# Layer 1's normalised patches two rows at a time in two buffers, filters and gated products alternating, transposes an iteration ahead of the projections; layer 2's corner weights in a PSUM bank

## The chip, the cores and the metric

One core of a Trainium2 chip runs the whole program, in float32. The metric is the device time of one execution in microseconds, as the median of several. Beside the timed runs there is one profiled execution, whose span and trace are read below. The engines are TensorE (PE, with its weight loads as PEld), VectorE (DVE), ScalarE (ACT), GpSimd (POOL) and SyncE (SP). SP, ACT and POOL issue DMAs.

## What is computed

Four images of 48 channels and 256 x 256 pixels go through four layers. Each layer adds to its input a function of the group-normalised input:

```python
x = x + L0(gn(x))   # 1x1 and 3x3 convolutions, product of 8x8 FFT patches, layer norm, gate, 1x1
x = x + L1(gn(x))
x = x + L2(gn(x))
x = x + L3(gn(x))   # 1x1, 3x3, gelu gate, 1x1, a filter on 8x8 FFT patches
```

The two layers that the change touches, cut to what matters:

```python
def L1(x):
    y = einsum('oc,bchw->bohw', w_in, x)              # 48 -> 288 channels
    f = rfft2(patches(y, 8)) * fft_mask               # a filter per channel on 8x8 patches
    y = unpatch(irfft2(f))
    y = depthwise_conv3x3(y, w_dw)
    x1, x2 = split(y, 2)
    return einsum('oc,bchw->bohw', w_out, gelu(x1) * x2)   # 144 -> 48

def L2(x):
    integ = cumsum(cumsum(x, -1), -2)                 # the table
    off   = conv1x1(gelu(conv3x3(x, w1_off)), w2_off)  # 4 offsets per pixel: a box
    scale = conv1x1(gelu(conv3x3(x, w1_mod)), w2_mod)  # 48 scales per pixel
    A, B, C, D = [bilinear(integ, corner) for corner in box(off)]
    return (A + D - B - C) / (area(off) * scale)
```

## The kernel before

**Two streams.** The program is written as two lists of work. Stream a does layers 0 and 1 of each image in turn, and then layer 3 of all images. Stream b does the first statistics, layer 1's weights in patch form (`patch_weights`), and then layer 2 of all images. Each layer is a Python generator, and `yield n` says that some n units of time have been written down; `run` always continues the stream whose sum of units is lower, so that both lists are mixed into one program. A layer waits until what it needs is written. So layer 2 of an image begins when its layer 1 has ended, and stands beside layer 0 and layer 1 of the next image; layer 2 of the last image stands beside layer 3. In the last loop of an image's layer 1, stream b has nothing to do. A scheduler at build time may then move instructions of one engine past one another, except those marked `pinned`. On the chip every engine takes its instructions in the fixed order that comes out.

Stream a issues its DMAs on SP (helper `dma`, L227), stream b on POOL; the column loads A and B of the convolutions go through SP or ACT. PSUM has eight banks of 128 x 512: stream a has a ring of five, stream b a ring of two and one bank of its own, `p2`.

**Layer 1** has three loops for each image.

1. *Patches times input weights* (L671 to L699), 16 strips of 8 rows in each half of the image. Two DMAs load the strip's rows into `xn`, one for each half of the image. One VectorE `tensor_scalar` (L679) normalises it and puts its pixels in patch order into `xp`. Then 32 matmuls (L688) with `win` follow, and 32 copies into `hs`, one half by VectorE (L693), the other by ScalarE (L695). One DMA stores `hs` (4608 KB) to `hD`. `xn` and `xp` have one buffer each, `hs` has two.
2. *Filter, 3x3 and gate* (L701 to L770), 72 groups of 4 channels. `fetch` loads `hg` (1024 KB) from `hD`, the filters `ct` and the 3x3 weights `tt` and `ht`, a group ahead. Four matmuls filter the group (L736), and their results are copied to `yt` by VectorE (L741) and ScalarE (L743). Six small transfers (`AROUND`) make `yh` from it, the rows that neighbouring patches need. For the group before, four matmuls multiply its patches (L758) and four its neighbours' rows (L759, accumulating); ScalarE's gelu (L762) and VectorE's product (L763) give `gt`, stored to `gD` every second group.
3. *Projection* (L772 to L808), 16 strips of four iterations. An iteration turns three blocks by four transposes each (L795), copies each block with ScalarE (L797) and multiplies it by the output weights (L798) right after its copy; VectorE adds the input `xt` (L800).

**Layer 2** first makes its table of sums. Then it goes through 32 pieces of eight rows for each image. `convolve` (L908) is the 3x3 convolution of a quarter piece, with ScalarE's gelu; `project` (L928) the 1x1 ones. Two quarters share the bank `p2`, and one VectorE addition (L935, 128 x 416) takes both out into `sc`. `boxes` (L946 to L993) makes of it, on VectorE, the corners, the gather's indices `idx`, the 16 weights for each pixel `w4` (L985) and the divisor. `gather` (L1000) issues from POOL 16 indirect DMAs for each tile `V` (three buffers), four to each of the four pixels a partition. `add` multiplies V by its weights in place (L1011, 128 x 3072, VectorE), adds the 16 corners in four halvings (L1013) and divides (L1014). `finish` turns the result on TensorE (L1025) and adds it to the image (L1032).

Of the kernel before, what the change touches and what calls it, by code (L numbers as in the profile page):

```python
# [11 lines left out]
ALU = mybir.AluOpType  # L12
# [176 lines left out]
class Net:  # L189
# [131 lines left out]
    def normalised_weights(self, wb, n, mr, pool):  # L321


        nc = self.nc
        t = self.column_scales(mr, pool)
        W = pool.tile([112, 4, n], F32, name=self.nm("W"), tag="W")
        md = pool.tile([112, 4], F32, name=self.nm("md"), tag="md")
        nc.vector.scalar_tensor_tensor(md[:], t[:, :, 0], -1.0, t[:, :, 1], ALU.mult, ALU.mult)
        mt = pool.tile([112, 4, 106], F32, name=self.nm("mt"), tag="mt")
        ps = self.bank()  # L330
        for g in range(4):
            k = 112 if g < 3 else 96
            nc.vector.tensor_scalar(W[:k, g, :], wb[:k, g, :], t[:k, g, 1:2], None, ALU.mult)
            nc.vector.tensor_scalar(mt[:k, g, :], self.tapsel[:k, g, :], md[:k, g : g + 1], None, ALU.mult)
        for g in range(4):
            k = 112 if g < 3 else 96
            nc.tensor.matmul(ps[:106, :n], mt[:k, g, :], wb[:k, g, :], start=g == 0, stop=g == 3)
        nc.vector.tensor_copy(W[96:106, 3, :], ps[96:106, :n])
        return W
# [318 lines left out]
    def layer1(self, x, mr, y):  # L658
# [4 lines left out]
        with ExitStack() as ctx:  # L663
            w = ctx.enter_context(self.pool("wa", 1))
            sb = ctx.enter_context(self.pool("ba", 2))

            win = w.tile([112, 288], F32, name="win")
            mh = w.tile([112, 2], F32, name="mh")
            xn = w.tile([112, 8, PW], F32, name="xn")
            xp = w.tile([112, 16, 128], F32, name="xp")  # L670
            nc.vector.memset(xn[32:64], 0.0)  # L671
            nc.vector.memset(mh[32:64], 0.0)
            for h in range(2):
                self.dma(win[64 * h : 64 * h + 48], a["L1_w_in"])
                self.dma(mh[64 * h : 64 * h + 48], mr[48 * h : 48 * h + 48])
            for s in range(NS):
                self.load_rows(xn, x, 8 * s, 8, 64)

                nc.vector.tensor_scalar(  # L679
                    xp[:].rearrange("p b (r c) -> p r b c", c=16),  # L680
                    xn[:, :, 1:257].rearrange("p r (b c) -> p r b c", c=16),
                    mh[:, 0:1], mh[:, 1:2], ALU.subtract, ALU.mult,
                )
                hs = sb.tile([128, 4 * NG, 2, 16], F32, name="hs", tag="hs")
                for b in range(16):
                    for h in range(2):
                        ps = self.bank()
                        nc.tensor.matmul(  # L688
                            ps[:, :288], xp[64 * h : 64 * h + 48, b, :], win[64 * h : 64 * h + 48],
                            start=True, stop=True,  # L690
                        )
                        if h:
                            nc.vector.tensor_copy(hs[:, :, h, b], ps[:, :288])  # L693
                        else:
                            nc.scalar.copy(hs[:, :, h, b], ps[:, :288])  # L695
                    if b == 7:
                        yield 13
                self.dma(hD[:, :, s, :], hs[:].rearrange("p (g c) h b -> p g (c h b)", c=4))
                yield 13  # L699
        with ExitStack() as ctx:  # L700
# [12 lines left out]
            todo, gt = None, None  # L713

# [13 lines left out]
            for g in range(NG + 1):  # L728
                if g < NG:
# [4 lines left out]
                    for c in range(4):  # L734
                        ps = self.bank()
                        nc.tensor.matmul(  # L736
                            ps[:].rearrange("p (s n) -> p s n", n=32), ct[:, c, :], hg[:, :, c, :],
                            start=True, stop=True,
                        )
                        if c % 2:  # L740
                            nc.vector.tensor_copy(pick(yt, 128, c), order(ps[:]))  # L741
                        else:
                            nc.scalar.copy(pick(yt, 128, c), order(ps[:]))  # L743
# [6 lines left out]
                if todo is not None:  # L750
                    go, yo, yho, to, ho = todo
                    if go % 2 == 0:
                        gt = sb.tile([128, NS, 4, 32], F32, name="gt", tag="gt")
                    for c in range(2):
                        both = []
                        for q in (c, c + 2):
                            ps = self.bank()
                            nc.tensor.matmul(order(ps[:]), to[:, q, :], pick(yo, 128, q), start=True, stop=False)  # L758
                            nc.tensor.matmul(order(ps[:]), ho[:, q, :], pick(yho, NZ, q), start=False, stop=True)  # L759
                            both.append(ps)  # L760
                        gl = sb.tile([128, 512], F32, name="gl", tag="gl")
                        nc.scalar.activation(gl[:], both[0][:], AF.Gelu)  # L762
                        nc.vector.tensor_mul(  # L763
                            gt[:, :, 2 * (go % 2) + c, :], gl[:].rearrange("p (s n) -> p s n", n=32),
                            both[1][:].rearrange("p (s n) -> p s n", n=32),
                        )
                    if go % 2:
                        self.dma(gD[:, :, go // 2, :], gt[:].rearrange("p s c n -> p s (c n)"))
# [3 lines left out]
        with ExitStack() as ctx:  # L772
# [5 lines left out]
            for h in range(2):  # L778
                self.dma(pr[:, h, 48 * h : 48 * h + 48], a["L1_w_out"][0:96, :])
                self.dma(pr[h:96:2, 2, 48 * h : 48 * h + 48], a["L1_w_out"][96:144, :])  # L780
            for s in range(NS):
                xt = sb.tile([CP, 8, PW], F32, name="xt", tag="xt")
                self.load_rows(xt, x, 8 * s, 8)
                gs = sb.tile([128, 144, 2, 16], F32, name="gs", tag="gs")
                self.dma(gs[:].rearrange("p c h b -> p (c h b)"), gD[:, s].rearrange("p g n -> p (g n)"))
                for j in range(4):
                    pp = self.bank()
                    for q in range(3):
                        pt = self.bank()
                        for b in range(4):  # L790
                            if q < 2:
                                of = gs[:, 0:96, q, 4 * j + b]
                            else:
                                of = gs[:, 96:144, :, 4 * j + b].rearrange("p c h -> p (c h)")
                            nc.tensor.transpose(pt[:96, 128 * b : 128 * b + 128], of, self.ident[:])  # L795
                        gc = sb.tile([96, 512], F32, name="gc", tag=f"gc{q}")
                        nc.scalar.copy(gc[:], pt[:96, :])  # L797
                        nc.tensor.matmul(pp[:CP, :], pr[:, q, :], gc[:], start=q == 0, stop=q == 2)  # L798
                    v = xt[:, :, 1 + 64 * j : 65 + 64 * j].rearrange("p r (b c) -> p b r c", b=4)
                    nc.vector.tensor_add(v, pp[:CP, :].rearrange("p (b r c) -> p b r c", b=4, r=8), v)  # L800
                    if j == 1:
                        yield 10
                for r in range(8):
                    nc.vector.bn_stats(st[:, 8 * s + r, :], xt[:, r, 1:257])
                self.store_rows(y, xt, 8 * s, 8)
                yield 10
# [67 lines left out]
    def layer2(self, x, mr, y, table):  # L874
# [3 lines left out]
        with ExitStack() as ctx:  # L878
# [15 lines left out]
            centre = self.load("c_centre", [128, 2, 512], w)  # L894
            kk = [112, 112, 112, 106]
# [26 lines left out]
            def project(t, j):  # L922

                if j % 2 == 0:
                    t.p2 = self.banks[self.stream].tile([128, 512], F32, name=self.nm("ps"), tag="p2", bufs=1)
                for b in range(4):
                    n = 52 * (4 * (j % 2) + b)
                    m = nc.tensor.matmul(  # L928
                        t.p2[:, n : n + 52], t.hm[j][:, 128 * b : 128 * b + 128], w2[:], start=True, stop=True
# [3 lines left out]
                if j % 2:  # L933
                    h = j // 2
                    self.pinned(nc.vector.tensor_add(  # L935
                        t.sc[:, 8 * h : 8 * h + 8, :], t.p2[:, 0:416].rearrange("p (k e) -> p k e", e=52),
                        b2[:].unsqueeze(1).to_broadcast([128, 8, 52]),
                    ))

            def boxes(t):  # L940
# [40 lines left out]
                w4 = sb.tile([128, 16, 4, 2, 2], F32, name="w4", tag="w4")  # L981
# [353 lines left out]
```

## Time and profile before

| what | value |
|---|---|
| median of 3 runs | 21125.43 us (21119.59 to 21126.28) |
| profiled execution | 21086.85 us |
| its span in the trace | 21084.9 us |
| layer 1 of image 0: loops 1, 2, 3 | 1971-2290, 2301-3185, 3203-3540 us |
| layer 1 of image 1: loops 1, 2, 3 | 5766-6245, 6262-7416, 7435-7775 us |
| layer 1 of image 2: loops 1, 2, 3 | 10015-10500, 10515-11686, 11704-12043 us |
| layer 1 of image 3: loops 1, 2, 3 | 14282-14770, 14781-15959, 15978-16317 us |
| layer 3 of three images beside layer 2 of the last | about 16430-20034 us |
| DMA | 3440 MB, mean 163 GB/s |

How to read it: layer 1 takes about 1.6 ms of an image without layer 2 beside it (image 0), and 2.0 ms with it. The times are those of one execution, from the span's start. A group's line gives the line number, the engine, the operation, the tile written and the tiles read, the shapes and the count; then busy us and the mean ns of one; then the idle time just before its instructions and what ended it. In a line of waits stand us in total, times, and the longest. In the timeline stand start and duration in us. "PEclk" or the granted clock is the share of TensorE's full clock that it was given. DMA share is the mean busy share of the 16 DMA engines.

### The profile page before, as it was taken

What the parts mean: (1) busy time and instruction counts of PE and PEld (TensorE: products, weight loads), DVE (VectorE), ACT (ScalarE), POOL (GpSimd) and SP (SyncE); (2) the same over time, 40 slices, a digit from 0 to 9 for tenths busy, and PEclk for the clock granted to TensorE, in tenths of its full rate; (3) what the DMA queues carried; (4) which work ended last, traced back from release to release, by engine and by line L of the source; (5) the groups of instructions that cost most, each with busy time, mean ns of one, the idle gap of its engine ahead of it and who ended that gap; (6) DMA issues with size and microseconds to landing.
All of it is one profiled execution on the core that took longest, in us unless ns stands there. A gap on an engine that the chain in (4) does not pass through costs nothing.

```text
span 21084.9 us, 230708 instructions
## 1 busy us (share of the span) xinstructions
PE 18992.2 (90%) x79032; PEld 12013.7 (57%) x79032; DVE 10675.3 (51%) x21479; ACT 5921.8 (28%) x12275; POOL 9864.3 (47%) x8887
## 2 busy tenths in 40 slices
PE   7998898999888879998888799997887899999999
PEld 4565434666443346665433466654334787878888
DVE  4544322476665534766655347667453245555521
ACT  2334212343331123433311234333112211111111
POOL 1000000277775602787755117777552067777700
PEclk9898899999868999999689999996889999999999
DMA  4624885555499955554989655549896566766633
GB/s 115 136 52 102 240 217 166 136 127 132 120 269 231 248 169 137 129 127 119 267 226 240 187 132 126 130 120 252 231 235 195 143 146 153 158 154 157 151 77 74
DMA packets 2420311, 3440.17 MB, mean 163 GB/s; under 512 B 573959, under 2 KB 1990895, under 8 KB 2302460
## 3 DMA queue, kind: packets, MB, share of 16 engines
q1 hardware_dynamic: 1883640, 2084.48, 38.2%
q0 software_dynamic: 452560, 1110.45, 21.4%
q10 hardware_dynamic: 82944, 230.48, 4.5%
q8 instruction: 635, 10.40, 0.2%
q14 instruction: 532, 4.35, 0.1%
HBM read 2486.99 MB, written 802.77 MB: 156 GB/s over the span
## 4 chain that ended last, share of the span: by engine, by line
PE 64%; DMA 12%; POOL 10%; DVE 5%; issue 5%; ACT 2%; SPq 1%; ACTq 0%; DVEq 0%; POOLq 0%
PE ps L426 20%; POOL V L1000 10%; PE ps L908 6%; PE ps L736 5%; PE ps L434 4%; PE ps L798 4%; PE ps L759 3%; DMA ct<-cD 3%; PE ps L758 3%; PE ps L1151 2%; PE ps L688 2%; DMA yh<-ys 2%; PE ps L847 2%; DMA A<-x 1%; ACT gc L797 1%
## 5 line engine op out<-in xcount | busy, mean ns | idle before, releaser
L1000 POOL DMA_INDIRECT V<-t,idx x8192 | 9453.9, 1154 | 3754.0 <-issue 2390.7
L426 PE MATMUL ps<-W,A 128*128 128x288 f32 (+1 forms) x24576 | 5574.7, 376 | 125.5 <-ACT o L531 45.6
L426 PEld LDWEIGHTS ps<-W,A 128*128 128x128 f32 x24576 | 4296.6, 192 | 1275.8 <-issue 517.7
L227 POOL DMA_DIRECT2D X<-x x192 | 145.1, 760 | 4408.7 <-DMA x<-xt 3129.8
L1013 DVE TENSOR_TENSOR V<-V 128x1536 f32<-128x1536 f32 (+3 forms) x2048 | 1841.2, 899 | 20.9
L1011 DVE TENSOR_TENSOR V<-V,w 128x3072 f32<-128x3072 f32 x512 | 1716.5, 3353 | 233.4 <-DMA V<-t,idx 213.0
L736 PE MATMUL ps<-hg,ct 128*128 128x512 f32 x2304 | 1255.2, 695 | 392.0 <-DMA ct<-cD 267.2
L908 PE MATMUL ps<-A,W 112*96 112x512 f32 x3072 | 1543.1, 641 | 13.9 <-DVE xt L1032 13.9
L507 ACT COPY qkv<-ps 128x288 f32<-128x288 f32 x2048 | 769.1, 401 | 2673.0 <-PE ps L426 1262.1
L759 PE MATMUL ps<-yh,ht 65*128 65x512 f32 x2304 | 1191.6, 663 | 207.8 <-DMA yh<-ys 190.8
L688 PE MATMUL ps<-win,xp 48*128 48x288 f32 x4096 | 1022.7, 578 | 336.5 <-DVE xp L679 168.1
L434 PE MATMUL ps<-W,B 58*128 58x288 f32 (+1 forms) x8192 | 1281.4, 392 | 29.7 <-DVE t L518 12.3
L530 DVE BATCH_NORM_STATS2 bs<-ps 128x6 f32<-128x96 f32 x2048 | 394.8, 251 | 1721.2 <-PE ps L528 1721.0
L1131 DVE TENSOR_TENSOR gp<-gl,ps 128x192 f32<-128x192 f32 x1024 | 353.5, 351 | 1672.7 <-ACT gl L1130 1671.9
L763 DVE TENSOR_TENSOR gt<-gl,ps 128x512 f32<-128x512 f32 x576 | 395.4, 687 | 1546.6 <-PE ps L759 1546.5
L736 PEld LDWEIGHTS ps<-hg,ct 128*128 128x128 f32 x2304 | 500.9, 225 | 1085.3 <-issue 1008.9
L758 PE MATMUL ps<-ys,tt 128*128 128x512 f32 x2304 | 1075.9, 608 | 9.1 <-ACT ys L743 9.1
L1130 ACT ACTIVATE gl<-ps 128x192 f32<-128x192 f32 x1024 | 333.5, 331 | 2539.1 <-PE ps L426 2220.0
L434 PEld LDWEIGHTS ps<-W,B 58*128 58x128 f32 x8192 | 765.9, 187 | 465.7 <-issue 355.5
L688 PEld LDWEIGHTS ps<-win,xp 48*128 48x128 f32 x4096 | 631.3, 253 | 694.1 <-ACT hs L695 211.8
L798 PE MATMUL ps<-gc,pr 96*96 96x512 f32 x1536 | 791.7, 625 | 210.4 <-ACT gc L797 195.8
L759 PEld LDWEIGHTS ps<-yh,ht 65*128 65x128 f32 x2304 | 459.0, 203 | 875.8 <-issue 770.1
(186 smaller groups left out, 24304.9 us busy)
## 6 DMA issues: line engine op xcount, KB each, us to landing
hD<-hs SPq DMA_DIRECT2D x64, 4608.0 KB
hg<-hD SPq DMA_DIRECT2D x288, 1024.0 KB
gD<-gt SPq DMA_DIRECT2D x144, 1024.0 KB
gs<-gD SPq DMA_DIRECT2D x64, 2304.0 KB
V<-t,idx POOLq DMA_INDIRECT x8192
A<-x SPq DMA_DIRECT2D x512, 193.5 KB
xt<-x SPq DMA_DIRECT2D x256, 387.0 KB
A<-x ACTq DMA_DIRECT2D x512, 193.5 KB
```

What stands on the lines that cost most here:

```text
L426: nc.tensor.matmul(to(q, b), A[:, r + q, 128 * b + g : 128 * b + g + 128], W[:, g, :], start=b == 0 and g == 0, stop=b == 1 and g == 2,)
L434: nc.tensor.matmul(to(q, b), B[p, r // 2, 128 * b : 128 * b + 128], W[p, 3, :], start=b == 1, stop=b == 0)
L507: nc.scalar.copy(t.qkv[:, 2 * q + b, :], banks[2 * b + q][:, 0:288])
L688: nc.tensor.matmul(ps[:, :288], xp[64 * h : 64 * h + 48, b, :], win[64 * h : 64 * h + 48], start=True, stop=True,)
L736: nc.tensor.matmul(ps[:].rearrange("p (s n) -> p s n", n=32), ct[:, c, :], hg[:, :, c, :], start=True, stop=True,)
L758: nc.tensor.matmul(order(ps[:]), to[:, q, :], pick(yo, 128, q), start=True, stop=False)
L759: nc.tensor.matmul(order(ps[:]), ho[:, q, :], pick(yho, NZ, q), start=False, stop=True)
L798: nc.tensor.matmul(pp[:CP, :], pr[:, q, :], gc[:], start=q == 0, stop=q == 2)
L908: m = nc.tensor.matmul(ps[:96, :].rearrange("p (r c) -> p r c", c=256), W[: kk[g], g, :], of[: kk[g]], start=g == 0, stop=g == 3,)
L1000: nc.gpsimd.indirect_dma_start(out=V[:, k, 4 * cr : 4 * cr + 4, :].rearrange("p e c -> p (e c)"), out_offset=None, in_=table, in_offset=ba ...
L1011: self.pinned(nc.vector.tensor_mul(Vm, Vm, wm.unsqueeze(2).to_broadcast([128, 64, 48])))
L1013: nc.vector.tensor_add(V[:, :, 0:n, :], V[:, :, 0:n, :], V[:, :, n : 2 * n, :])
```

## The change

In layer 1's first loop `xn` becomes two buffers of two rows, `xp` two buffers of a whole strip. A strip's rows are loaded and normalised in four steps of two rows (eight DMAs and four `tensor_scalar` where there were two and one), and the next strip's are written down in the middle of a strip. In the second loop, two filters, two gated products, two filters and two gated products of the group before take turns, and the `yh` transfers come after both. In the third loop the transposes of an iteration are written ahead of the projection of the iteration before. In layer 2 every quarter's projection has a bank of the ring and its own addition (128 x 208), and the bank that was `p2` holds two sets of the weights `w4`. `normalised_weights` takes `mt` from a pool that it gives back. The pieces' operations are otherwise as they were.

```diff
-            xn = w.tile([112, 8, PW], F32, name="xn")
-            xp = w.tile([112, 16, 128], F32, name="xp")
+            xns = [w.tile([112, 2, PW], F32, name=self.nm("xn")) for _ in range(2)]
+            xps = [w.tile([112, 16, 128], F32, name=self.nm("xp")) for _ in range(2)]
...
+            def normalise(s):
+                for r in range(0, 8, 2):
+                    xn = xns[r // 2 % 2]
+                    self.load_rows(xn, x, 8 * s + r, 2, 64)
+                    nc.vector.tensor_scalar(
+                        xps[s % 2][:].rearrange("p b (r c) -> p r b c", c=16)[:, r : r + 2],
+                        xn[:, :, 1:257].rearrange("p r (b c) -> p r b c", c=16),
+                        mh[:, 0:1], mh[:, 1:2], ALU.subtract, ALU.mult,
+                    )
+            normalise(0)
             for s in range(NS):
-                self.load_rows(xn, x, 8 * s, 8, 64)
-                nc.vector.tensor_scalar(
...
                     if b == 7:
+                        if s + 1 < NS:
+                            normalise(s + 1)
                         yield 13
                 self.dma(hD[:, :, s, :], hs[:].rearrange("p (g c) h b -> p g (c h b)", c=4))
                 yield 13
...
+                for c in range(2):
+                    if g < NG:
+                        filtered(2 * c)
+                        filtered(2 * c + 1)
+                    if todo is not None:
+                        gated(c)
...
+            def turn(s, j):
...
+                for q in range(3):
+                    pt = self.bank()
...
+                        nc.tensor.transpose(pt[:96, 128 * b : 128 * b + 128], of, self.ident[:])
+                    gc = sb.tile([96, 512], F32, name="gc", tag=f"gc{q}")
+                    nc.scalar.copy(gc[:], pt[:96, :])
+                    got.append(gc)
+                return got
+            def project(s, j, got):
...
+                for q in range(3):
+                    nc.tensor.matmul(pp[:CP, :], pr[:, q, :], got[q][:], start=q == 0, stop=q == 2)
...
+                for j in range(4):
+                    got = turn(s, j)
+                    if last is not None:
+                        project(*last)
+                    last = (s, j, got)
+                    yield 5
+            project(*last)
...
+            weights = self.banks[self.stream].tile([128, 2, 256], F32, name=self.nm("w4"), tag="w4", bufs=1)
...
-                if j % 2 == 0:
-                    t.p2 = self.banks[self.stream].tile([128, 512], F32, name=self.nm("ps"), tag="p2", bufs=1)
+                ps = self.bank()
...
+                self.pinned(nc.vector.tensor_add(
+                    t.sc[:, 4 * j : 4 * j + 4, :], ps[:, 0:208].rearrange("p (k e) -> p k e", e=52),
+                    b2[:].unsqueeze(1).to_broadcast([128, 4, 52]),
+                ))
...
-                w4 = sb.tile([128, 16, 4, 2, 2], F32, name="w4", tag="w4")
+                w4 = weights[:, (2 * s + i) % 2].rearrange("p k (c i j) -> p k c i j", c=4, i=2, j=2)
```

## Prediction

> **What bounds the kernel now.** I read, in this order, the page's first part and its chain, the busy time by stage (windows), the waits of TensorE in single stages, the gathers' group beside VectorE's, and the timeline of one strip. The page names TensorE:
>
> ```profile
> PE 18992.2 (90%) x79032; PEld 12013.7 (57%) x79032; DVE 10675.3 (51%) x21479; ACT 5921.8 (28%) x12275; POOL 9864.3 (47%) x8887
> PE 64%; DMA 12%; POOL 10%; DVE 5%; issue 5%; ACT 2%; SPq 1%; ACTq 0%; DVEq 0%; POOLq 0%
> ```
>
> But the change touches stages with other limits, so the stages are what I price. Columns of the windows: stretch, its length, busy us of PE, PEld, DVE, ACT and POOL with counts, granted clock, DMA share, GB/s. The rows are layer 1's first loop (patches times `win`) of image 0 and of image 1, its second and third loops of image 1, a stretch of layer 0 beside layer 2, and layer 3 beside layer 2.
>
> ```profile
> 1971.00:2290.00 319.00, 204.57 (x1024) 159.39 (x1024) 173.31 (x271) 152.17 (x256) 0.00 (x0) 0.70 1.02 270
> 5766.00:6245.00 479.00, 396.86 (x1360) 218.63 (x1360) 354.19 (x570) 168.69 (x276) 381.64 (x321) 0.68 0.98 267
> 6262.00:7416.00 1154.00, 1018.79 (x2344) 436.79 (x2344) 594.12 (x873) 194.56 (x321) 677.46 (x645) 0.89 0.93 237
> 7435.00:7775.00 340.00, 284.89 (x1165) 153.36 (x1164) 107.47 (x212) 106.22 (x192) 2.20 (x4) 0.98 0.57 177
> 4217.00:5700.00 1483.00, 1409.27 (x5555) 881.44 (x5554) 1032.47 (x2292) 589.99 (x1241) 1176.34 (x988) 0.98 0.51 126
> 16900.00:19900.00 3000.00, 2907.28 (x18089) 2408.59 (x18088) 1636.10 (x2881) 558.27 (x1255) 2275.00 (x2007) 0.98 0.69 154
> ```
>
> The first loop is bound by DMA (1.02 and 0.98), and TensorE, waiting in it, is granted only 0.70 and 0.68 of its clock. The second is nearly DMA's. The third is TensorE's, at 84% busy. In the last two rows TensorE is 95 to 97% busy.
>
> **First loop: normalised patches two rows at a time.** Removed: the wait of a strip's matmuls for its own normalised rows,
>
> ```profile
> PE ps L688 <- DVE xp L679: 100.6, 15, 12.1
> PE ps L688 <- DVE xp L679: 23.0, 6, 5.4
> ```
>
> (us in total, times, longest; image 0, then image 1). It buys nothing by itself, because DMA's time stays: image 0's 319 us over 16 strips are 19.9 us a strip for one 4608 KB store of `hs` and two 387 KB loads, and 5382 KB in 19.9 us is the row's 270 GB/s. Images 1 to 3 take 479/16 = 29.9 us, gathers included.
>
> Added is a dependence. There were 2 loads a strip, now 8 of 97 KB into two buffers, so rows 4 to 7 cannot be loaded before VectorE has normalised rows 0 to 3. All stand on SP's queue with the store. The order of the changed program shows: in image 0 the four normalises of strip s+1 stand after 13 to 16 of strip s's 16 VectorE copies, and in images 1 to 3 in their midst; SP has a store behind all loads of the next strip, and there also behind the first half of the strip after. The VectorE instruction that waits for a load holds up the copies behind it, and these hold up the store.
>
> Image 0, the loop from store to store: the store's bytes, 4608/5382 of 19.9 us = 17.0; rows 0 to 3 behind it, 1.4; landing, about 2 (an estimate from the gathers, whose multiply starts no earlier than 1.8 us after they end); one normalise, a quarter of 1360 ns, and three copies of 641 ns, 2.3. Sum 22.7, so +2.8 a strip, +45 us. Images 1 to 3: a store issued at 5907.35 lets the next x flow from 5928.2 to 5936.1, so 20.9; half of x, 4.0; from then to the strip's last copy the program order holds some 8 us of VectorE work (the copies left and layer 2's box sums among them). Sum 33, +3 a strip, +48 an image. In all +190. Bounds: -30 (DMA saturated as before and the last 2% gained) and +400, if the halves behind both turn serial (a loop of about 38 us).
>
> Here a rule of the Trainium skill speaks against the edit: "SBUF — State Buffer", The DMA setup-cost knee, puts some 2 us of fixed cost on a transfer and asks for the largest single one. Taken literally, 8 loads for 2 add 6 x 2 = 12 us a strip, +770 us over 64 strips. The row says less: loads that are queued together share the landing (30 loads and 16 stores in 479 us still ran at 267 GB/s), so only the second round trip is new; I take the sum above.
>
> **Second loop: filters and gated products alternate.** Same instructions: per group 4 filter matmuls (L736), 4 L758, 4 L759, 4 copies, the 6 small `yh` transfers. TensorE's waits in image 1 are transfers, not copies:
>
> ```profile
> PE ps L759 <- DMA yh<-ys: 65.9, 20, 7.7
> PE ps L736 <- DMA ct<-cD: 55.1, 18, 6.7
> ```
>
> so smoothing the evacuations gains nothing that is seen. The built order is two filters, two L758, again, then four L759. `yh` is issued after the last filter's copy, now two matmuls (2 x 0.9 us at the granted clock) later than before relative to its reader. If each of the 20 waits grows by 1.8 us it is +36 an image; SP's queue of issues paces the loop and takes up most. I take +8 an image, +30. Bounds -40 and +140.
>
> **Third loop: transposes one iteration ahead of the projections.** Removed is this wait:
>
> ```profile
> PE ps L798 <- ACT gc L797: 48.8, 74, 0.7
> PE ps L795 <- DMA gs<-gD: 18.3, 1, 18.3
> ```
>
> The first line goes: one iteration's 12 transposes (3 x 4) run while ScalarE copies, 106.22/64 = 1.7 us of copying in a 4.4 us iteration. The second, the loop's start, stays. Layer 2 does not run here (POOL 2.20), so what TensorE saves is saved on the path: 340 less 48.8 is 291, less a little for `gs` now asked for later against its reader: -44 an image, -175. Bounds -120 and -220.
>
> **Layer 2: sums per quarter, weights in PSUM.** 256 additions of 587 ns (L935, 128x416) become 512 of half the size. From 128x512 at 687 ns and 128x416 at 587, a column costs 1.04 ns and the start 154, so 370 ns: +39 us of VectorE, which is 70% busy there; hidden. Without that cover it is +39. On the ring of two banks the projections now stand with the convolutions (L908) and transposes, and a convolution may wait for an addition that stands behind a 3.4 us multiply and 3.6 us of additions on VectorE. TensorE's waits for the ring are 13.9 us now (L908); four times as many is nearest: +40. Bounds 0 and +120.
>
> The multiply (L1011) now reads one operand from PSUM. Its own time I leave, 3353 ns. But see what it does to the gathers:
>
> ```profile
> 5905.77 0.94 POOL L1000 DMA_INDIRECT V<-t,idx  x1 [0.30 <-issue]
> 5907.01 7.21 POOL L1000 DMA_INDIRECT V<-t,idx  x1 [0.30 <-issue]
> 5907.14 3.34 DVE L1011 TENSOR_TENSOR V<-V,w 128x3072 f32<-128x3072 f32 x1
> 5914.52 0.95 POOL L1000 DMA_INDIRECT V<-t,idx  x1 [0.30 <-issue]
> L1000 POOL DMA_INDIRECT V<-t,idx x8192 | 9453.9, 1154 | 3754.0 <-issue 2390.7
> L1011 DVE TENSOR_TENSOR V<-V,w 128x3072 f32<-128x3072 f32 x512 | 1716.5, 3353 | 233.4 <-DMA V<-t,idx 213.0
> ```
>
> A gather takes 0.95 us, and 7.2 when it meets the multiply. The groups hold 8192 x (1154 - 947) = 1.7 ms of such excess. By the operation running at a gather's start, 1.1 ms are the multiply's (2.15 us each), 0.44 ms the additions' (L1013), which stay.
>
> The Trainium skill has two sentences on this in "SBUF — State Buffer", Who interferes with whom: a VectorE instruction with two SBUF inputs contends with a GpSimd one that reads SBUF, and one with a single SBUF input doesn't; and, as an inference, that `tensor_tensor` leaves descriptor generation alone. By the second nothing changes; by the first each multiply lets POOL go. The trace agrees with the first, so POOL gains up to 1.1 ms of its own time. What is that worth? In 4217:5700 POOL is at 1176 us busy plus 0.30 us a gather, 1462 of 1483, and it waits for a free V buffer for under 10 us: one V, from multiply to multiply, takes 24.1 us there, its 16 gathers 23.7 of them. So POOL sets the pace together with TensorE. TensorE's own excess over dense matmuls is about 105 us in this stretch, part of it layer 0's own chain; VectorE waits 40.6 us for V. I take 36 us per 1483, over 5,100 us of layer 0 beside layer 2 in three images: -125. Bounds 0 and -360 (all 105). Beside layer 3 the V buffers are ready 37 us ahead of their multiply, so nothing.
>
> **Sum.** +190 +30 -175 +40 -125 = -40 us on the profiled execution of 21086.85 us (span 21084.9), 21047. The median is 38.6 us above it, so 21,085 for the median of 21125.4.
>
> **Rivals.** (1) The first loop turns serial, slower: its one mechanism is a normalise that waits in VectorE's queue while the store waits for the copies behind it. At 38 us a strip in images 1 to 3 and 25 in image 0 it is +390 +80 = +470 in place of +190, and the sum +240: 21,365; halfway, +100: 21,225. It decides from about 34 us a strip on (4 us x 48 strips = +190, with image 0 +235, balances the rest). For it speaks that VectorE is 74% busy in this loop; against it, that gathers use the DMA time that falls free. (2) POOL was the pacer: 2.15 us fewer per V would let a V go by in 21.9 us, and all 105 us per stretch go, -360 in place of -125, and the sum is -275: 20,850. For it: POOL waits for nothing; against: TensorE is 95% busy. (3) The PSUM operand doesn't free POOL (the second sentence): +85, 21,210.
>
> **Numbers.** Forecast case (sum between -150 and +30, 20,975 to 21,155) 0.40; rival 1, 0.24; rival 2, 0.24; rival 3, 0.12. A measurement of this kernel tells about 0.2%, 42 us, from no change. Of the forecast case half lies below -42 and the rest mostly within; rival 2 is all faster; rivals 1 and 3 are mostly slower. Faster 0.48, same 0.20, slower 0.32. The range reaches from rival 2 to rival 1's middle: 20,830 to 21,290; the likeliest case's own is 20,975 to 21,155.
>
> **What would show it.** Right: strips of the first loop at about 23 and 33 us with DMA share below 0.95; the third loop near 297 us without the `gc` wait; the second within 10 us; gathers at the multiply at 0.95 us, and a V every 23.5 us beside layer 0. Wrong: a first loop above 34 us a strip or unchanged; gathers still held; new waits of L947 (the convolution) for the additions above 100 us.

## The result, and the profile after

The changed kernel takes 20881.15 us (20858.34 to 20892.74, 4 runs) against 21122.51 us for the kernel before (21104.32 to 21126.28, 4 runs). The ratio is 0.9886, 95% interval 0.9869 to 0.9903: faster by 1.1%, 241 us. The profiled execution took 20882.08 us, 205 less than the one of before.

The page of the changed kernel, its engines and the chain that ended last. In busy time almost nothing moves but POOL, from 9864 us to 8637. In the chain POOL goes from 10% to 7%, DMA from 12% to 15% and VectorE from 5% to 7%:

```profile
PE 18892.3 (90%) x79032; PEld 12001.4 (57%) x79032; DVE 10763.0 (52%) x21931; ACT 5909.3 (28%) x12275; POOL 8637.2 (41%) x8887
PE 65%; DMA 15%; DVE 7%; POOL 7%; issue 4%; SPq 1%; ACT 1%; DVEq 0%; ACTq 0%; POOLq 0%
```

The stages say where the time went. These are the windows of the changed kernel for the same six pieces of work, with the same columns as before: first loop of image 0 and of image 1, second and third loop of image 1, layer 0 beside layer 2, layer 3 beside layer 2.

```profile
1983.00:2340.00 357.00, 206.13 (x1024) 158.56 (x1024) 182.42 (x316) 153.78 (x256) 0.00 (x0) 0.67 0.86 242
5699.00:6252.00 553.00, 410.44 (x1360) 225.30 (x1360) 360.25 (x624) 170.21 (x276) 304.49 (x315) 0.64 0.80 229
6269.00:7425.00 1156.00, 1016.97 (x2344) 432.87 (x2343) 600.25 (x888) 194.94 (x321) 609.29 (x642) 0.90 0.91 236
7445.00:7738.00 293.00, 263.23 (x1161) 152.12 (x1159) 108.40 (x227) 100.54 (x191) 5.20 (x8) 0.95 0.71 213
4217.00:5650.00 1433.00, 1396.91 (x5542) 874.60 (x5542) 1037.95 (x2297) 589.69 (x1237) 1021.73 (x995) 0.99 0.53 131
16700.00:19700.00 3000.00, 2908.29 (x18068) 2405.97 (x18067) 1646.45 (x2930) 556.97 (x1254) 1973.74 (x2008) 0.98 0.67 154
```

In the first loops the DMA share falls from 1.02 and 0.98 to 0.86 and 0.80: for the same bytes they take longer. In the third loop a wait is gone. In the fifth row about the same work, 5542 matmuls against 5555, takes 1433 us instead of 1483, and POOL is busy 155 us less.

Taken from the two traces, from the first to the last matmul of one line (us): for the first loop the line of its matmuls (L688, in the changed kernel L697), for the second the filters (L736, L728), for the third the projections (L798, L828):

| part | before, images 0 to 3 | after, images 0 to 3 | sum of changes | forecast |
|---|---|---|---|---|
| first loop | 305, 469, 473, 472 | 343, 542, 542, 542 | +250 | +190 |
| second loop | 869, 1137, 1151, 1154 | 874, 1142, 1148, 1129 | -18 | +30 |
| third loop | 333, 341, 339, 339 | 277, 280, 280, 279 | -236 | -175 |
| up to the first loop (layer 0; in images 1 to 3 beside layer 2) | 1971, 2228, 2238, 2237 | 1983, 2165, 2176, 2173 | +12, -63, -62, -64 | -85 for all of layer 2 |
| after the last third loop (layer 3, and layer 2 beside it) | 4766 | 4758 | -8 | 0 |

The rest of the 205, about 16 us, lies in what these stretches leave out, the gaps between the loops and the loops' first and last groups. With its transposes and the gap before it, the third loop gains 238 us.

The gathers and the multiply, as the page has them (busy us, mean ns, idle us before):

```profile
L1037 POOL DMA_INDIRECT V<-t,idx x8192 | 8227.0, 1004 | 4897.9 <-issue 2346.8
L1048 DVE TENSOR_TENSOR V<-V,w 128x3072 f32<-128x3072 f32 x512 | 1713.3, 3346 | 35.9 <-DMA V<-t,idx 27.0
```

A gather is down from 1154 ns to 1004, the multiply is as long as before, and VectorE's waits for V fell from 213 us to 27. The timeline of the changed kernel shows why: a multiply, and the gathers that start during it.

```profile
5897.17 3.33 DVE L1048 TENSOR_TENSOR V<-V,w 128x3072 f32<-128x3072 f32 x1
5897.93 0.95 POOL L1037 DMA_INDIRECT V<-t,idx  x1 [0.30 <-issue]
5899.18 0.95 POOL L1037 DMA_INDIRECT V<-t,idx  x1 [0.30 <-issue]
5900.43 0.94 POOL L1037 DMA_INDIRECT V<-t,idx  x1 [0.30 <-issue]
5901.68 1.79 POOL L1037 DMA_INDIRECT V<-t,idx  x1 [0.30 <-issue]
```

Two lie wholly inside the multiply and take 0.95 us. The first long one, 1.79 us, comes after it, during the first of the additions. Over the whole trace, 441 gathers of the kernel before began while a multiply ran; their median is 3.48 us, and 422 of them ended only after it. In the changed kernel 928 did so; their median is 0.95 us, and 689 ended within it.

### The profile page after: what moved, and what is told of

It is laid out like the page before. It is cut to its first block, busy times and chain, and to the rows that moved or that the text cites. A ratio compares the mean times of both kernels' runs of the same rounds, so it can differ in the third digit from the quotient of the medians.

```text
span 20880.3 us, 231985 instructions
## 1 busy us (share of the span) xinstructions
PE 18892.3 (90%) x79032; PEld 12001.4 (57%) x79032; DVE 10763.0 (52%) x21931; ACT 5909.3 (28%) x12275; POOL 8637.2 (41%) x8887
## 3 DMA queue, kind: packets, MB, share of 16 engines
q0 software_dynamic: 452560, 1110.45, 21.1%
## 4 chain that ended last, share of the span: by engine, by line
PE 65%; DMA 15%; DVE 7%; POOL 7%; issue 4%; SPq 1%; ACT 1%; DVEq 0%; ACTq 0%; POOLq 0%
PE ps L427 19%; POOL V L1037 7%; PE ps L947 6%; PE ps L728 5%; PE ps L435 4%; PE ps L741 4%; DMA ct<-cD 4%; PE ps L742 3%; PE ps L697 3%; PE ps L828 3%; DMA hD<-hs 2%; PE ps L1188 2%; DVE V L1050 2%; PE ps L815 1%; PE ps L966 1%
## 5 line engine op out<-in xcount | busy, mean ns | idle before, releaser
L1037 POOL DMA_INDIRECT V<-t,idx x8192 | 8227.0, 1004 | 4897.9 <-issue 2346.8
L1048 DVE TENSOR_TENSOR V<-V,w 128x3072 f32<-128x3072 f32 x512 | 1713.3, 3346 | 35.9 <-DMA V<-t,idx 27.0
L728 PE MATMUL ps<-hg,ct 128*128 128x512 f32 x2304 | 1264.4, 676 | 417.5 <-DMA ct<-cD 339.5
L947 PE MATMUL ps<-A,W 112*96 112x512 f32 x3072 | 1544.9, 642 | 26.2 <-DVE xt L1069 21.5
L697 PE MATMUL ps<-win,xp 48*128 48x288 f32 x4096 | 1054.8, 594 | 547.9 <-DVE xp L684 232.4
L741 PE MATMUL ps<-ys,tt 128*128 128x512 f32 x2304 | 1174.1, 632 | 27.6 <-DVE ys L732 25.7
L697 PEld LDWEIGHTS ps<-win,xp 48*128 48x128 f32 x4096 | 647.3, 259 | 924.3 <-ACT hs L704 291.9
L728 PEld LDWEIGHTS ps<-hg,ct 128*128 128x128 f32 x2304 | 468.0, 211 | 1051.6 <-issue 949.1
L947 PEld LDWEIGHTS ps<-A,W 112*96 112x96 f32 x3072 | 513.9, 176 | 731.4 <-issue 690.3
```

The lines of the kernel that those rows point to most:

```text
L697: nc.tensor.matmul(ps[:, :288], xp[64 * h : 64 * h + 48, b, :], win[64 * h : 64 * h + 48], start=True, stop=True,)
L728: nc.tensor.matmul(ps[:].rearrange("p (s n) -> p s n", n=32), ct[:, c, :], hg[:, :, c, :], start=True, stop=True)
L947: m = nc.tensor.matmul(ps[:96, :].rearrange("p (r c) -> p r c", c=256), W[: kk[g], g, :], of[: kk[g]], start=g == 0, stop=g == 3,)
L1037: nc.gpsimd.indirect_dma_start(out=V[:, k, 4 * cr : 4 * cr + 4, :].rearrange("p e c -> p (e c)"), out_offset=None, in_=table, in_offset=ba ...
L1048: self.pinned(nc.vector.tensor_mul(Vm, Vm, wm.unsqueeze(2).to_broadcast([128, 64, 48])))
```

## The experiments

Times in the text are medians in us; loops and stretches are taken from a kernel's one profiled execution, in the way of the table. Each kernel was timed beside the kernel before, on one chip. A comparison with the changed kernel goes across chips: the kernel before took 21,116 and 21,127 us beside these kernels, and 21,122.5 beside the changed one. For four of the runs (the late normalise, the first runs of the two buffers of four rows and of layer 2 alone, and the eight loads into two buffers) the chip granted TensorE about 0.85 of its clock instead of 0.92, to the kernel before too, which took 25,197 and 25,277 us there. Of these I read the first loop of image 0, which no layer 2 accompanies and in which DMA sets the time (307 us there in the kernel with layer 2 alone, whose first loop is that of before: 305), and the ratio; what was expected of images 1 to 3 and of the totals cannot be read from them. Where the first loop is that of before, image 0's takes 302 to 307 us in five traces, so 5 us there can be chance.

**First loop as before.** The hunk of the first loop taken back:

```diff
-            xns = [w.tile([112, 2, PW], F32, name=self.nm("xn")) for _ in range(2)]
-            xps = [w.tile([112, 16, 128], F32, name=self.nm("xp")) for _ in range(2)]
+            xn = w.tile([112, 8, PW], F32, name="xn")
+            xp = w.tile([112, 16, 128], F32, name="xp")
```

> The changed kernel with layer 1's first loop as it was before. Theory S (the loads split in four are a pure loss, whatever else was changed): the first loops go back to 305 and 470 us from 343 and 542, in all -250 us, so about 20,630, 0.977 of before. Rival T (the slower first loop only moves work: stream b gets ahead in it, and the stretch beside layer 0 is the shorter for it): the first loops gain 250, but the stretches between third loop and first loop grow from 2,170 us again toward 2,235, and the total stays within 60 us of 20,880.

Measured: 20651.36 (20640.12 to 20677.06), ratio to before 0.9783 (0.9767 to 0.9799), 230 us below the changed kernel. The first loops take 305, 483, 479 and 483 us, the stretches up to them 2174, 2171 and 2173. Theory S holds, and T falls: nothing is given back. Images 1 to 3 stay some 10 us above the 471 of before: probably the gathers, faster now, take more of DMA beside this loop; no run shows it.

**Weights back in SBUF.** One tile moved, nothing else:

```diff
-                w4 = weights[:, (2 * s + i) % 2].rearrange("p k (c i j) -> p k c i j", c=4, i=2, j=2)
+                w4 = sb.tile([128, 16, 4, 2, 2], F32, name="w4", tag="w4")
```

> The changed kernel with the weights w4 in SBUF again, two buffers; the bank stays empty, the quarter sums and the ring as changed. Theory P (the multiply with two SBUF operands held the gathers, and POOL set the pace beside layer 0): gathers mean 1154 ns again, a V every 24.1 us beside layer 0 instead of 23.4, three stretches +60 us each, total +190: 21,070. Rival Q (the finer sums and the ring let TensorE and VectorE run more freely, the weights' place does not matter): within 40 us of 20,880, and the stretches stay at 2,170.

Measured: 21117.97 (21079.44 to 21147.29), ratio 1.000 (0.9991 to 1.0009), 237 us above the changed kernel. The stretches are back at 2233, 2240 and 2230, and the first loops of images 1 to 3 are 20 longer (564, 559, 565). The group in this run's page:

```profile
L1036 POOL DMA_INDIRECT V<-t,idx x8192 | 9372.0, 1144 | 4076.1 <-issue 2379.6
L1047 DVE TENSOR_TENSOR V<-V,w 128x3072 f32<-128x3072 f32 x512 | 1717.5, 3355 | 219.7 <-DMA V<-t,idx 201.3
```

1144 ns a gather, 201 us of waiting for V and a V every 24.2 us beside layer 0, as before the change. So theory P, and Q falls: the quarter sums and the ring without the weights' new place are worth nothing. All that layer 2 gains comes from the place of one operand of 512 instructions, which themselves are no faster for it. The instructions that write the weights moved with them, but are not the cause: of the 1.6 ms by which this kernel's gathers exceed 947 ns each, those that began during such a write hold 1 us, and those that began during a multiply 1046 us.

**Second loop as before.** The four filters first, then the gated products, as before.

> The changed kernel with layer 1's second loop as it was before. Theory A (transfers pace it, the order of the matmuls is worth nothing): second loops within 10 us each of the changed kernel's 874 and 1,140, total within 30 us of 20,880. Rival B (alternating shortens TensorE's waits for yh): image 3's second loop goes back from 1,129 to 1,154, the others by as much, total +20 to +80.

Measured: 20859.23 (20824.43 to 20870.33), ratio 0.9873 (0.9857 to 0.989); the second loops take 871, 1125, 1144 and 1129. Theory A: the order is worth nothing that can be told (22 us below the changed kernel, across chips). In particular the 25 us that image 3 gained are there without the alternation.

**Third loop as before.** The projection's matmul again right behind its block's copy.

> The changed kernel with layer 1's third loop as it was before. Theory C (the wait of the projection for its copy was on the path, and TensorE ran its first matmul after it slowly besides): third loops 338 us instead of 279, total +235: 21,115. Rival D (what the third loop gains is given back at the start of the next layer, where first loads are late): total less than +120.

Measured: 21118.84 (21089.69 to 21171.36), ratio 1.0005 (0.9998 to 1.0012), 238 above the changed kernel, with third loops of 334, 339, 340 and 339. Theory C: 238 for the 235 expected; nothing is given back.

**Next strip's loads after the copies.** To find what in the first loop costs, the call is moved:

```diff
                     if b == 7:
-                        if s + 1 < NS:
-                            normalise(s + 1)
                         yield 13
                 self.dma(hD[:, :, s, :], hs[:].rearrange("p (g c) h b -> p g (c h b)", c=4))
+                if s + 1 < NS:
+                    normalise(s + 1)
                 yield 13
```

> The changed kernel with the next strip's loads and normalises written down after the strip's copies and store, not in its middle; still eight loads and four normalises. Theory V (VectorE's queue: copies stand behind normalises that wait, and the store behind the copies): first loops fall from 343/542 to about 310/485, total about 20,680. Theory R (the second round trip, rows 4 to 7 waiting for rows 0 to 3, with SP's queue): they stay above 335/530, total within 50 us of 20,880.

Measured beside a kernel before of 25,197 us: ratio 1.0125 (1.0106 to 1.0144); image 0's first loop takes 382 us, longer than the changed kernel's 343. Its window:

```profile
1972.00:2360.00 388.00, 191.40 (x1024) 138.19 (x1024) 173.92 (x317) 149.35 (x256) 0.00 (x0) 0.67 0.75 211
```

The DMA share is down to 0.75. TensorE's waits for normalised rows in this window are seven of up to 27 us:

```profile
PE ps L697 <- DVE xp L684: 189.1, 7, 27.1
```

In seven of the strips a normalise waits 16 us for rows whose load stands behind a store. That is R's second round trip, and writing the loads early had hidden a part of it. V's forecast fails, since the loop is worse although no normalise among the copies waits more than 1.6 us from the third strip on. R had said only that the loop would not get shorter.

**Two buffers of four rows.** Four loads and two normalises a strip:

```diff
-            xns = [w.tile([112, 2, PW], F32, name=self.nm("xn")) for _ in range(2)]
+            xns = [w.tile([112, 4, PW], F32, name=self.nm("xn")) for _ in range(2)]
...
-                for r in range(0, 8, 2):
-                    xn = xns[r // 2 % 2]
-                    self.load_rows(xn, x, 8 * s + r, 2, 64)
+                for r in range(0, 8, 4):
+                    xn = xns[r // 4]
+                    self.load_rows(xn, x, 8 * s + r, 4, 64)
```

The second halves of a strip need not wait for the first here, and there are two normalises for four. Beside the slower-clocked kernel of before, and then again beside one of 21127.05 us:

> The changed kernel with two buffers xn of four rows, four loads of 194 KB and two normalises a strip, in the middle of the strip before; no rows wait for another rows' normalise within a strip. To find the room, five small temporaries of the box sums have one buffer. Theory R: first loops 310/490. Theory V: above 335/530.

> Two buffers xn of four rows, four loads and two normalises a strip, as in the earlier run of it, where image 0's first loop took 313 us. Theory R: 313 in image 0 and about 490 in images 1 to 3, total about 20,700. Theory V: images 1 to 3, where VectorE has layer 2's work between the normalises and the copies, stay above 530, total above 20,830.

Measured first: ratio 0.9956 (0.9939 to 0.9973), image 0's first loop 313. Again: 20645.69 (20625.2 to 20658.67), ratio 0.977 (0.9756 to 0.9785), first loops 313, 483, 478 and 473. So R's numbers, in images 1 to 3 too. VectorE's normalises still stand in the middle of its copies there, but they hardly wait any more (below).

**One load.** Two loads of eight rows and one normalise, still ahead of its strip and into two buffers `xp`. With two buffers for every temporary of the box sums this kernel does not fit into SBUF (72 KB of a partition, 70.9 left); here and in the kernels with buffers of four rows, five small ones have one.

> The changed kernel with one buffer xn of eight rows, two loads and one normalise a strip, in the middle of the strip before, into two buffers xp; five small temporaries of the box sums have one buffer. Theory V (copies behind a waiting normalise): first loops stay near 343/542, total near 20,880. Theory R (only the second round trip of the split loads costs): 305 to 315 and 480, total about 20,650. Rival of both (the second buffer of xp pays once loads are whole): below 300/470, total below 20,620.

Measured: 20630.33 (20606.69 to 20645.4), ratio 0.9759 (0.9744 to 0.9774); first loops 300, 479, 472 and 472. R's numbers again; below neither bound of the third case. Against the first loop as before (305, 483, 479 and 483) it is 4 to 11 us a loop and 21 in all, across chips, and so no more than chance. The window of image 0's first loop in this kernel, DMA full again (1.03) and TensorE at 0.70 of its clock, with two buffers `xp` as with one:

```profile
1970.00:2285.00 315.00, 207.89 (x1024) 163.31 (x1024) 175.83 (x272) 154.20 (x256) 0.00 (x0) 0.70 1.03 271
```

The same of the kernel with four loads, at 0.93:

```profile
1970.00:2295.00 325.00, 210.18 (x1026) 163.56 (x1026) 180.42 (x294) 154.14 (x257) 0.00 (x0) 0.68 0.93 257
```

And of the next kernel, with eight loads into the two buffers, at 0.92:

```profile
1983.00:2310.00 327.00, 203.77 (x1024) 155.91 (x1024) 176.44 (x286) 153.59 (x256) 0.00 (x0) 0.69 0.92 258
```

**Eight loads into two buffers.** Is it the number of loads?

```diff
+                    for q in range(0, 4, 2):
+                        self.load_rows(xn[:, q : q + 2], x, 8 * s + r + q, 2, 64)
```

> Two buffers xn of four rows, but each filled by four loads of two rows: eight loads a strip as in the changed kernel, two normalises, and no rows that wait for another rows' normalise within the strip. Theory R (the second round trip is the cost): first loops as with four loads, 313 and 480, total about 20,650. Rival N (the number of loads is the cost: each brings its own fixed time and its turn on the queue's semaphores): 335 and more in image 0, 520 and more in images 1 to 3, total about 20,830.

Measured beside a kernel before of 25,277 us: ratio 0.9978 (0.9968 to 0.9989); image 0's first loop 318 us with eight loads, where four took 313 and the changed kernel's eight take 343. So the number of loads is worth about 5 us in a loop (64 more loads, 0.08 us each), no more than equal loops differ by. Ending the wait of rows for rows is worth 25, with two normalises for four.

**The order that was built.** These kernels differ in VectorE's order too, since the scheduler places a normalise where it finds room. A stretch of the changed kernel in image 0, behind thirteen of a strip's sixteen copies:

```profile
2127.72 0.55 DVE L684 TENSOR_SCALAR xp<-xn,mh 112x512 f32<-112x512 f32 x1 [6.39 <-DMA xn<-x]
2128.18 1.11 DVE L702 COPY hs<-ps 128x288 f32<-128x288 f32 x2
2129.14 0.52 DVE L684 TENSOR_SCALAR xp<-xn,mh 112x512 f32<-112x512 f32 x1
2129.58 0.63 DVE L702 COPY hs<-ps 128x288 f32<-128x288 f32 x1
2130.84 0.52 SPq L227 DMA_DIRECT2D hD<-hs  x1
```

In thirteen of the sixteen strips a normalise waits so, 4.5 to 6.4 us, for rows that queue behind a store; the strip's last three copies stand behind it, and the next store behind these. The stores are 22.1 to 23.2 us apart. With four loads, two copies stand so in every second strip; the stores are 23 us apart there and 17.7 in the strips between. With one load none does from the third strip on, and the stores are 19.5 us apart on average (19.4 before).

Counted from the traces, copies whose matmul had ended stood behind a normalise that waited for its rows (us in a first loop):

| kernel | held in image 0 | loop of image 0 | held in images 1 to 3 | loops of images 1 to 3 |
|---|---|---|---|---|
| the changed kernel | 73 | 343 | 58 to 60 | 542 |
| eight loads, two buffers of four rows | 32 | 318 | | |
| four loads, two buffers of four rows | 25 | 313 | 6 to 8 | 473 to 483 |
| one load | 1 | 300 | 14 to 17 | 472 to 479 |
| late normalises | 6 | 382 | | |

So a kernel that ends the wait of rows for rows also frees most of the held copies. The runs show that the two-row buffers, with their four normalises, are the cost, and the last row shows that the second round trip costs time with the copies free. How much of the changed kernel's cost is V's is not shown.

**Layer 2 alone.** The kernel before with the changed layer 2:

> The kernel before with layer 2 of the changed kernel alone (quarter sums, weights in PSUM). Theory P: three stretches beside layer 0 shorter by 60 us each, first loops of images 1 to 3 longer by about 12 each since the gathers take more of DMA, total -150 to -190: 20,950, 0.992 of before. Rival: the gain needs the other parts, total within 40 us of before.

> The kernel before with the changed layer 2 alone. Where TensorE is granted 0.92 of its clock on average, theory P expects the stretches beside layer 0 shorter by 60 us each and the total at -150 to -190, 0.992 of before. Where it is granted 0.85, as in the earlier run of it, TensorE is slower than POOL throughout, and no gain is expected.

Measured first, beside 25,197 us: ratio 0.9997 (0.9986 to 1.0009), nothing. Again, beside 21127.05: 20923.55 (20910.32 to 20938.67), ratio 0.9904 (0.9889 to 0.9919), -204 us; stretches 2171, 2174 and 2169. In the first of these runs, in a stretch of layer 0 beside layer 2 (4217:5700), the longest of POOL's waits was:

```profile
POOL V L999 <- DVE res L1013: 383.7, 22, 26.8
```

TensorE's, in the same stretch of the same run:

```profile
PE ps L426 <- issue: 98.6, 60, 16.5
PE ps L434 <- issue: 62.5, 29, 9.5
```

POOL stood 384 of 1483 us waiting for a V to be used, and TensorE stood 161 us with nothing to wait for that the trace shows. A V went by every 32.3 us there, where POOL needs 24.1 even when it is held. Where TensorE is the slower of the two, freeing POOL gives nothing; that fits theory P from its other side.

**What paid, without the rest.** First and second loops as before, third loop and layer 2 as changed:

> The changed kernel with layer 1's first and second loops as before: of the change, the third loop and layer 2 are left. Should be the sum of what paid: third loops -235, stretches beside layer 0 -190, first loops of images 1 to 3 some 30 longer for the faster gathers, against before -430 to -480: 0.978 of before, 20,650; the second loop alone is worth 20 us or less either way.

Measured: 20644.98 (20626.27 to 20680.21), ratio 0.9773 (0.976 to 0.9787). It beats both kernels, as do the others in which no rows wait for rows (20,630 to 20,651, all within 0.1% of each other).

## Why the prediction came out as it did

The total was in the range and on the side forecast, but 204 us below the stated 21,085: the gain forecast, 40 us, is a sixth of the measured 241, and rival 2's 20,850 came nearest. Two gains were taken too small, and one cost. That the total is no further off is luck: the first loop cost 60 us more than forecast and the third loop gained 61 more, and these cancel. What is left is layer 2 (-197 in the table for -85) and the second loop (-18 for +30).

*What POOL's time is worth* is the term that was most mis-sized: -125 in the sum, -189 in the three stretches, and some -60 more in first loops. I took 36 us in 1483, since TensorE was 95% busy and only 105 us seemed open. It was 50, and 63 for each of the three stretches: a V every 23.3 us, where I had said 23.5. Rival 2 had put all 105 there, so the truth lies between the two, and its total came nearest with the help of the terms that cancel. The sign that I had read and not followed was POOL's own row: 1462 of 1483 us occupied, and under 10 us of waiting for a buffer. Its longest wait in 4217:5700 of the kernel before is the gap between gathers:

```profile
POOL V L1000 <- issue: 285.3, 936, 0.3
```

So POOL held the pace here although TensorE's busy share was the higher one; that share has its own slack in it (it stands at 97% after). After the change POOL waits for VectorE to release a V, as these waits of the changed kernel in 4217:5650 show:

```profile
POOL V L1037 <- issue: 281.1, 922, 0.5
POOL V L1037 <- DVE res L1051: 70.9, 18, 8.6
```

There is also a place that I left out: in the changed kernel's first loops of images 1 to 3 the freed gathers are worth 20 us each (564 with the weights in SBUF, 542 without), where I had expected nothing. Of the two sentences of the Trainium skill ("SBUF — State Buffer", Who interferes with whom) the first decides here: with one operand in PSUM the multiply no longer holds a gather. The inference that `tensor_tensor` spares descriptor generation gives the wrong answer for these gathers, 1144 ns against 1004; which part of a gather is held, no run here shows. Of what is left above 947 ns, 8192 x 57 ns = 0.47 ms, the gathers that began during an addition, whose operands both stay in SBUF, hold 0.31 ms (0.40 before, where I had 0.44). And the 7.21 us that I showed are not the multiply's alone: that gather began 0.13 us before the multiply and ended 3.7 us after it, while a normalise and two additions ran.

*The third loop* gained 236 us and not 175, by the mechanism that I named. The groups of the four third loops, of the kernel before and then of the changed one:

```profile
L798 PE MATMUL ps<-gc,pr 96*96 96x512 f32 x1536 | 791.7, 625 | 210.4 <-ACT gc L797 195.8
L795 PE MATMUL ps<-c_ident_sb,gs 128*96 128x128 f32 x3072 | 429.0, 276 | 73.2 <-DMA gs<-gD 73.2
L828 PE MATMUL ps<-gc,pr 96*96 96x512 f32 x1536 | 719.1, 605 | 3.8 <-ACT gc L817 3.8
L815 PE MATMUL ps<-c_ident_sb,gs 128*96 128x128 f32 x3072 | 407.6, 282 | 136.3 <-DMA gs<-gD 115.2 <-ACT gc L817 21.1
```

So the wait went (-207), and the projections' and transposes' own busy time fell by 73 and 21, which I had not counted; why it fell is not shown (the ends of matmuls are modelled, so that a busy time can hold some waiting). What came back is the late `gs` and a wait of the transposes for a copy, +63. The sum is -238.

*The first loop* cost what I had said by the loop that I had said, and in image 0 its size was close: stores 22.1 to 23.2 us apart for a sum of 22.7, and +2.4 us a strip of 2.8 forecast. In images 1 to 3 it was +4.4 a strip (212 us over 48 strips), not 3. The runs keep the second round trip (four rows to a buffer end most of the cost). They do not settle what I had hung beside it, VectorE's copies behind a waiting normalise: in image 0 the trace shows them on the way from store to store, as the sum has it, and no kernel here takes them away and leaves the rest as it was. Rival 1 didn't come, but by little: it needed 38 us a strip, its threshold was about 34, and 33.9 came in images 1 to 3. The Trainium skill's rule on large transfers ("SBUF — State Buffer", The DMA setup-cost knee) would have charged 12 us a strip for the six more loads, 8 of them for the step from four to eight; that step cost about 5/16 = 0.3 us.

*The second loop* was forecast at +30 and is within what can be told from nothing. In image 1 the waits moved from `yh` to `ct`:

```profile
PE ps L728 <- DMA ct<-cD: 73.1, 21, 7.4
PE ps L742 <- DMA yh<-ys: 37.8, 13, 8.2
```

It was 55.1 for `ct` and 65.9 for `yh` before. Over the four images, in the groups of the filters and of the neighbours' rows, the idle time that `yh` ended fell from 229 us to 127, and what `ct` ended rose from 267 to 340. When a queue of transfers paces a loop, its waits change names.

*The ring of two banks* came as taken in its parts: the waits of the convolutions and projections for it (L947 and L966 on the image's addition and the sums) are 59.5 us in the page's groups, where 14 stood before, +45 for a forecast of 40; and the additions are 371 ns (370). Little of it reaches the end: the kernel with the weights in SBUF has this ring and these sums, and its stretches beside layer 0 (2233, 2240, 2230) are those of before. So the +40 of the sum was not paid.

## What to carry to other kernels

Ask of each engine how long it waits for its consumer, not only how busy it is: one that hardly waits can be the one that sets the pace, as POOL did here at 79% busy beside a TensorE at 95%. An instruction can be worth moving an operand for what it does to another engine, without getting faster itself. And a transfer-bound loop takes small loads well and dependent loads badly: a buffer that makes row 4 wait for row 0 costs a round trip in each strip, and the second buffer behind it did not pay that back. Look at the order that was built before a difference between two kernels is put down to the lines that were moved.

## What the runs showed of the hardware

Most gathers that POOL begins during a VectorE multiply of two SBUF operands end only after it (422 of 441, median 3.48 us in place of 0.95); with one operand in PSUM most end within it (689 of 928, median 0.95), and the multiply takes 3346 ns against 3353. Small loads in a row cost about 0.08 us each beyond their bytes (5 us for 64 loads), which can be chance here. And one program took 21.1 ms on one chip and 25.2 on another, with a granted clock of 0.92 and 0.85; the 19% are more than the clock's 8%, and the time in which TensorE waited for nothing that the trace shows (161 us in 1483, in the kernel with layer 2 alone) is where to look for the rest. It was not followed further.
